# A four-layer graph attention kernel: the rows of layer 3's heads 1 to 3 from bf16 parts

## The chip, the core and the metric

The kernel runs on one core of a Trainium2 chip. The metric is the device time of one execution in microseconds (us), as the median of several runs. The core's engines are named as in the profile: PE is TensorE (matmul) and PEld its weight loads, DVE is VectorE, ACT is ScalarE, POOL is GpSimd and SP is SyncE.

## The reference

Four layers of graph attention work on 16 graphs of 1024 nodes with 256 features and an adjacency matrix. Each layer normalises x, projects it, and mixes the nodes with weights that depend on an edge's two ends. Layer 3 has four heads of 64 features:

```python
# x: (16, 1024, 256) f32; adj: (16, 1024, 1024), 0 or 1
h = jnp.maximum(_layernorm(x, axis=-1), 0.0)
# layers 0 to 2, one head each, with an activation of their own:
e = act(f1[:, :, None] + f2[:, None, :])         # f1 = Wh @ a1, f2 = Wh @ a2
attention = softmax(where(adj == 0, NEG, e))
x = x + einsum('bij,bjo->bio', attention, Wh)    # elu of it in layers 1 and 2
# layer 3, four heads (h: head, e: feature):
h = jnp.einsum('bnd,hde->bhne', x_normed, W)
weight = leaky_relu(e_src[..., :, None] + e_dst[..., None, :])
attention = softmax(where(adj == 0, NEG, weight))
out = relu(einsum('bhij,bhje->bhie', attention, h) + bias) + h
x = x + layernorm(out)                           # for each head
```

The weight of an edge (i, j) is thus a function of a number of i and a number of j. The kernel works with their exponentials, so a weight is the maximum (in one layer the minimum) of two numbers, times the mask of edges. One number runs along the partitions, the other along the free axis and has to stand on all partitions. This second one is "the row" below.

## The kernel before

The 16 graphs are called batches. Two streams run batches alternately, the even ones and the odd ones, as Python generators; a driver takes the stream that is behind by the times that the generators yield (`yield 3.6`, `yield 0.5`), and so interleaves their program order. A scheduler then orders the instructions of each engine by readiness and priority. `tc.keep_in_program_order(ins)` ties an instruction behind the one that was traced just before it on the same engine; it adds no wait on another engine. Each engine then works through its order, and waits where an input isn't there.

For every layer of a batch, and in layer 3 for every head:

- `weigh` (L306) takes the only `row` buffer in PSUM (`bufs=1`[...]), which both streams share, guarded by `row_taken`. For each of the eight blocks of 128 nodes it turns a column of 128 numbers into 128 elements of the row: one f32 transpose on PE with the column broadcast over 128 columns (L314), so that the row stands on all 128 partitions.
- It then makes eight tiles `weights` of 128x1024 on DVE (L318), each from the row, a number for each partition and a mask. The last one gives the row back.
- In layers 0 to 2, `attend` multiplies the weights with the values V (L409). `add_elu` or `finish0` evict, and `project` prepares the next layer: it centres (L274), squares on ACT (L281), transposes into a `misc` buffer in PSUM (L290), copies it to `hT` on ACT (L292), and multiplies by W (L297).

In layer 3 the columns come from `ex` (L381), which holds three groups of four heads for each block. Products go through PE in tiles of 32 columns, four side by side (L519): `add_values` for the values and `add_totals` for the sums of weights. For head 0, the values come in two blocks with `yield 3.6` behind each. Only then `weigh3(1)` begins and the row of head 1 is turned, and the totals of head 0 follow. For heads 1 to 3, the next head's row is turned before the head's own totals and values. After each head ACT copies both accumulators (L581), PE turns them back in the two `misc` buffers (L588, L596), and DVE and POOL normalise.

The lines that matter below: L88 (`ones`, used at L244 alone), L314, L318, L506 to L512 (`weigh3`), and L547 to L565, the start of the loop over heads.

Of the kernel before, what the change touches and what calls it, by code (L numbers as in the profile page):

```python
# [32 lines left out]
F32 = mybir.dt.float32  # L33
BF = mybir.dt.bfloat16
# [7 lines left out]
P = 128  # L42
# [5 lines left out]
SLOPE = 0.2  # L48
L3_SLOPE = 0.01

REACH = 75.0


# [6 lines left out]
def short_path(ctx: ExitStack, tc: tile.TileContext, ins: dict, out: bass.AP, bad: bass.AP):  # L60

    nc = tc.nc
# [22 lines left out]
    make_identity(nc, ident)  # L85
    minus_half = const.tile([P, 1], F32, name="minus_half")
    nc.vector.memset(minus_half, -0.5)
    ones = const.tile([P, P], F32, name="ones")  # L88
    nc.vector.memset(ones, 1.0)

    squares = const.tile([P, B, NI], F32, name="squares")
    inverses = const.tile([P, B, NI], F32, name="inverses")
# [69 lines left out]
    def prepare():  # L162

        forms = [
            (SLOPE, 1 - SLOPE, SLOPE - 1),
            (-SLOPE, SLOPE - 1, 1 - SLOPE),
            (0.0, 1.0, -1.0),
            (L3_SLOPE, 1 - L3_SLOPE, L3_SLOPE - 1),  # L170
        ]
        scratch = [edges.tile([P, N], F32, name="weights1") for _ in EXT]

        def extend(l: int):
            n = EXT[l] // 3
            engine = nc.vector if l == 0 else nc.gpsimd
            for c, factor in enumerate(forms[l]):
                engine.tensor_scalar_mul(
                    W[l][:, :, D + c * n : D + (c + 1) * n],
                    wa[:, :, l : l + n, 0 if c == 2 else 1],  # L180
                    factor,
                )

        def fetch(l: int):
            def begin(dst: bass.AP, src: bass.AP):
                fetched = nc.sync.dma_start(dst, src)
                if l > 0:
                    tc.keep_in_program_order(fetched)

            if l < 3:  # L190
                begin(W[l][:, :, :D], ins[f"L{l}_W"].rearrange("(k p) o -> p k o", p=P))
                begin(scratch[l][:, : 2 * D], on_all_partitions(ins[f"L{l}_a"], 2 * D))
                return
            for k in range(NK):
                begin(
                    W[3][:, k, :D].rearrange("p (h e) -> p h e", h=H),
                    ins["L3_W"][:, ts(k, P), :].rearrange("h p e -> p h e"),
                )
            for s, name in enumerate(("L3_a_src", "L3_a_dst")):
                first = ins[name]  # L200
                begin(
                    scratch[3][:, ts(s, D)].rearrange("p (h e) -> p h e", h=H),
                    bass.AP(tensor=first.tensor, offset=first.offset, ap=[[0, P], [T * E, H], [1, E]]),
                )
            for t, a in ((bias, ins["L3_bias"]), (gamma, ins["L3_gamma"]), (beta, ins["L3_beta"])):
                begin(t, on_all_partitions(a, D))

        for l in range(3):
            fetch(l)
            yield  # L210
            for k in range(NK):
                for s in range(2):
                    prod = work.tile([P, D], F32, name="above", bufs=2)
                    made = nc.vector.tensor_tensor_reduce(
                        prod, W[l][:, k, :D], scratch[l][:, ts(s, D)], op0=ALU.mult, op1=ALU.add,
                        scale=1.0, scalar=0.0, accum_out=wa[:, k, l, s : s + 1],
                    )
                    if l > 0:
                        tc.keep_in_program_order(made)
            extend(l)  # L220
            yield
        fetch(3)
        yield
        for s in range(2):
            for k in range(NK):
                prod = work.tile([P, D], F32, name="above", bufs=2)
                tc.keep_in_program_order(
                    nc.vector.tensor_mul(prod, W[3][:, k, :D], scratch[3][:, ts(s, D)])
                )
                nc.vector.tensor_reduce(  # L230
                    wa[:, k, 3:, s], prod.rearrange("p (h e) -> p h e", h=H), AX.X, ALU.add
                )
        extend(3)

        tc.keep_in_program_order(nc.vector.tensor_scalar_add(beta, beta, -2.0))
        tc.keep_in_program_order(nc.vector.tensor_scalar_mul(gamma, gamma, ROOT_E))

        groups = (3 + H) * 2
        wa2 = small.tile([P, NK, groups], F32, name="wa2", bufs=1)
        nc.vector.tensor_mul(wa2, wa.rearrange("p k g s -> p k (g s)"), wa.rearrange("p k g s -> p k (g s)"))  # L240
        norms = psum.tile([P, 3 + H, 2], F32, name="misc")
        for k in range(NK):
            nc.tensor.matmul(
                norms.rearrange("p g s -> p (g s)"), ones, wa2[:, k],  # L244
                start=(k == 0), stop=(k == NK - 1),
            )
        both = small.tile([P, 3 + H], F32, name="both", bufs=1)
        nc.vector.tensor_reduce(both, norms, AX.X, ALU.add)
        worst = small.tile([P, 1], F32, name="worst", bufs=1)
        nc.vector.tensor_reduce(worst, both, AX.X, ALU.max)  # L250
        nc.vector.tensor_scalar(bad, worst, REACH * REACH / (2.0 * D), None, op0=ALU.is_gt)
        yield
# [50 lines left out]

    row_taken = []

    def weigh(b: int, column, c, op, into: list):  # L306


        while row_taken:
            yield 0.25  # L310
        row_taken.append(b)
        r = psum.tile([P, N], F32, name="row", bufs=1)
        for i in range(NI):
            nc.tensor.transpose(r[:, ts(i, P)], column(i).to_broadcast([P, P]), ident)  # L314
        yield 0.5
        for j in range(NI):
            w = edges.tile([P, N], F32, name=f"weights{b % 2}")
            nc.vector.scalar_tensor_tensor(w, r, c(j), masks[b][:, j // 2, :, j % 2], op0=op, op1=ALU.mult)  # L318
            into.append(w)
            if j == NI - 1:  # L320
                row_taken.pop()
            yield 0.5

    def start(behind, b: int):

# [23 lines left out]
    def batch(b: int):  # L349
# [43 lines left out]
        def attend(l: int, V: bass.AP, finish, then: int):  # L393

            weights = []
            behind = weigh(
                b, lambda i: V[:, i, D + 2 : D + 3], lambda j: V[:, j, D + 1 : D + 2],
                ALU.min if l == 1 else ALU.max, weights,
            )
            yield from start(behind, b)  # L400
            following = begin(then) if then < 3 else begin3()
            steps = iter(())
            accs = {}
            sums = small.tile([P, NI], F32, name="sums_of_x")

            def product(i: int, j: int):
                if j == 0:
                    accs[i] = accumulator(b)[:, : D + 1]
                nc.tensor.matmul(  # L409
                    accs[i], weights[j][:, ts(i, P)], V[:, j, : D + 1],  # L410
                    start=(j == 0), stop=(j == NI - 1),
                )


            for j in range(NI):
                next(behind)
                product(0, j)
                product(1, j)
                if b == 0 and j == NI - 1:


                    next(preparing)
                    if l == 0:
                        next(loading[1])
                    next(preparing, None)
                yield 0.9
            for _ in behind:
                pass
            for i in range(NI):
                if i > 1:  # L430
                    for j in range(NI):
                        product(i, j)
                acc = accs.pop(i)
                finish(i, acc, sums[:, i : i + 1])
                if i != 0:
                    yield 3.6
                if i % 2 == 1:

                    yield from steps
                    steps = project(b, then, xb, sums, i // 2, following[1])  # L440
                yield from islice(steps, 1)
            yield 1.0
            yield from steps
            return following[0]
# [61 lines left out]
        def weigh3(h: int):  # L506
            if h == H:
                return iter(())
            return weigh(
                b, lambda i: ex[:, i, 2 * H + h : 2 * H + h + 1],  # L510
                lambda j: ex[:, j, H + h : H + h + 1], ALU.max, weights,
            )  # L512

# [32 lines left out]

        behind = weigh3(0)  # L547
        yield from start(behind, b)
        for h in range(H):


# [2 lines left out]
            if h == 0:  # L554
# [6 lines left out]
                    yield 3.6  # L561
                for _ in behind:
                    pass
            behind = weigh3(h + 1)
            yield from start(behind, b)  # L565

# [447 lines left out]
```

## Time and profile before

| | before |
|---|---|
| time, median of 3 runs | 2988.73 us (2987.17 to 2989.75) |
| f32 turns for rows, layers 0 to 2 | 384, 273 ns median in the records |
| f32 turns for rows, layer 3 | 512, 273 ns median |
| weight loads of these turns | 137 ns median |
| one tile of weights on DVE | 1275 ns median |
| TensorE clock granted | 0.99 of full speed |

The records of matmuls overlap[...]. How long PE is taken up is read from the distance of two starts instead. For the f32 turns in one row this distance is 109 ns, less than half of the 273 ns in the record. The first one of a group has to wait for its own weight load.

The timeline, the windows and the chain of waits give the rest: the first shows when each row is made and what follows it, the second which engine is full in a stretch, and the third what the end depends on.

### The profile page before, as it was taken

How to read it: one execution, taken by the hardware profiler on the slowest of the kernel's cores; microseconds unless marked ns; L12 is line 12 of the kernel's file. 1: busy time of each engine (PE TensorE's matmuls, PEld its weight loads, DVE VectorE, ACT ScalarE, POOL GpSimd, SP SyncE). 2: the span in 40 equal slices, each digit the busy share in tenths (PEclk: the TensorE clock that was granted, in tenths of full speed). 3: DMA queues.
4: the chain of work that ended last, by engine and by line, in shares of the span. 5: the costliest groups of instructions: out<-in, count | busy, mean ns of one | idle time of the engine just before them, and what ended most of it. 6: DMA issues, size and time to landing. Idle time of an engine off the chain costs nothing.

```text
span 2988.9 us, 44636 instructions
## 1 busy us (share of the span) xinstructions
PE 2839.7 (95%) x16774; PEld 1986.1 (66%) x16774; DVE 2148.9 (72%) x4467; ACT 1090.0 (36%) x3009; POOL 956.7 (32%) x1455
## 2 busy tenths in 40 slices
PE   7999999999999999999999999999999999999985
PEld 5775856768576685766758566685766857667552
DVE  5658688585976859678586885859768586785855
ACT  2333434343343433424334243433434334343331
POOL 2123324243242423424233242432424233242333
PEclk9999999999999999999999999999999999999987
DMA  7204122040221303122041220302213031110101
GB/s 122 39 8 60 33 29 57 8 50 29 30 56 17 55 16 50 36 29 57 5 51 32 29 57 8 50 29 32 55 17 59 11 50 36 15 29 6 25 18 26
DMA packets 120495, 106.11 MB, mean 36 GB/s; under 512 B 73680, under 2 KB 91216, under 8 KB 120272
## 3 DMA queue, kind: packets, MB, share of 16 engines
q0 software_dynamic: 40448, 67.12, 15.4%
q1 hardware_dynamic: 79824, 36.05, 5.8%
q8 instruction: 135, 2.21, 0.3%
q14 instruction: 88, 0.72, 0.1%
HBM read 153.49 MB, written 33.55 MB: 63 GB/s over the span
## 4 chain that ended last, share of the span: by engine, by line
PE 55%; DVE 28%; issue 8%; POOL 5%; ACT 3%; DMA 1%; POOLq 0%; SPq 0%; ACTq 0%; DVEq 0%
PE acc L409 33%; DVE weights L318 19%; PE acc L297 9%; PE acc L519 9%; PE misc L290 2%; POOL rstd L261 2%; POOL y L487 1%; ACT square L281 1%; DVE x_b L345 1%; DVE V L365 1%; PE row L314 1%; DVE x_b L344 1%; ACT below L341 1%; DVE y L488 1%; DVE var L496 1%
## 5 line engine op out<-in xcount | busy, mean ns | idle before, releaser
L409 PE MATMUL acc<-V,weights 128*128 128x257 f32 x6144 | 1436.6, 385 | 26.2 <-DVE weights L318 15.7
L409 PEld LDWEIGHTS acc<-V,weights 128*128 128x128 f32 x6144 | 1143.3, 191 | 262.0 <-DVE weights L318 68.5
L318 DVE SCALAR_TENSOR_TENSOR weights<-row,ex,mask 128x1024 f32<-128x1024 f32 x512 | 630.3, 1273 | 102.5 <-PE row L314 95.7
L519 PE MATMUL acc<-weights,V 128*32 128x512 f32 x6144 | 692.1, 597 | 11.4 <-DVE weights L318 7.5
L297 PE MATMUL acc<-W,hT 128*128 128x259 f32 (+1 forms) x2048 | 521.6, 391 | 40.4 <-ACT hT L292 28.9
L297 PEld LDWEIGHTS acc<-W,hT 128*128 128x128 f32 x2048 | 379.0, 191 | 148.3 <-ACT hT L292 35.1
L318 DVE SCALAR_TENSOR_TENSOR weights<-row,V,mask 128x1024 f32<-128x1024 f32 x384 | 473.9, 1275 | 0.7 <-PE row L314 0.7
L519 PEld LDWEIGHTS acc<-weights,V 128*32 128x32 f32 x6144 | 189.4, 110 | 422.9 <-issue 415.3
L341 ACT ACTIVATE below<-acc,inv 128x256 f32<-128x256 f32 x256 | 120.8, 472 | 798.9 <-DVE inv L334 559.5
L281 ACT ACTIVATE square<-x_b,minus_mean 128x256 bf16<-128x256 f32 x512 | 259.7, 507 | 230.8 <-DVE minus_mean L271 155.0
L261 POOL TENSOR_TENSOR rstd<-rstd,minus_half 128x2 f32<-128x2 f32 (+1 forms) x320 | 302.0, 944 | 20.3
L389 POOL TENSOR_TENSOR x_b<-x_b,beta 128x256 f32<-128x256 f32 x128 | 93.4, 730 | 490.9 <-ACT square L281 490.9
L260 POOL TENSOR_SCALAR rstd<-squared 128x2 f32<-128x2 f32 x256 | 57.7, 225 | 573.2 <-ACT square L281 572.3
L333 DVE TENSOR_SCALAR inv<-acc 128x1 f32<-128x1 f32 x256 | 39.3, 154 | 277.6 <-PE acc L409 276.4
L344 DVE SCALAR_TENSOR_TENSOR x_b<-below,x_b 128x256 f32<-128x256 f32 x256 | 136.8, 534 | 82.7 <-ACT below L341 82.5
L292 ACT ACTIVATE hT<-misc 128x512 f32<-128x512 f32 x256 | 150.0, 592 | 119.9 <-PE misc L290 119.5
L361 ACT ACTIVATE V<-acc,rstd 128x3 f32<-128x3 f32 x384 | 98.5, 262 | 251.7 <-PE acc L297 250.8
L581 ACT COPY sums<-acc 128x512 f32<-128x512 f32 x128 | 74.8, 585 | 278.6 <-PE acc L519 278.6
L365 DVE TENSOR_SCALAR V<-acc,rstd,V 128x256 f32<-128x256 f32 x256 | 131.7, 538 | 62.2 <-ACT V L361 61.3
L290 PE MATMUL misc<-ident,centered 128*128 128x128 f32 x1024 | 158.7, 277 | 15.7 <-DVE centered L274 13.9
L274 DVE TENSOR_SCALAR centered<-x_b,minus_mean 128x256 f32<-128x256 f32 x512 | 168.5, 357 | 5.2
L290 PEld LDWEIGHTS misc<-ident,centered 128*128 128x128 f32 x1024 | 121.3, 141 | 60.1 <-issue 26.9
(76 smaller groups left out, 2218.1 us busy)
## 6 DMA issues: line engine op xcount, KB each, us to landing
adj_i<-in_adj_dram POOLq DMA_DIRECT2D x128, 256.0 KB, 3.9
x_b<-in_x_dram SPq DMA_DIRECT2D x16, 1024.0 KB, 6.4
narrow<-in_adj_dram POOLq DMA_DIRECT2D x64, 256.0 KB, 9.3
out_dram<-y POOLq DMA_DIRECT2D x32, 512.0 KB, 7.4
mask<-narrow SPq DMA_TRANSPOSE x64, 4.4
W<-in_L_gnn_W_dram SPq DMA_DIRECT2D x3, 256.0 KB, 7.2
weights<-in_L_gnn_a_dram SPq DMA_DIRECT2D x3, 256.0 KB, 8.5
W<-in_L_gnn_W_dram SPq DMA_DIRECT2D x2, 128.0 KB, 8.2
```

The costliest lines, as they stand in the source:

```text
L261: nc.gpsimd.tensor_tensor(r, r, minus_half.to_broadcast([P, n]), op=ALU.pow)
L274: nc.vector.tensor_scalar(centered[:, n, :], xb[:, 2 * pair + n, :], minus_mean[:, n : n + 1], 0.0, op0=ALU.add, op1=ALU.max,)
L281: nc.scalar.activation(square, xb[:, 2 * pair + n, :], AF.Square, bias=minus_mean[:, n : n + 1], accum_out=squared[:, n : n + 1],)
L290: nc.tensor.transpose(turned[:, k, ts(n, P)], centered[:, n, ts(k, P)], ident)
L292: nc.scalar.mul(hT, turned, ROOT_D)
L297: nc.tensor.matmul(projected, hT[:, k, ts(n, P)], W[l][:, k, :], start=(k == 0), stop=(k == NK - 1),)
L318: nc.vector.scalar_tensor_tensor(w, r, c(j), masks[b][:, j // 2, :, j % 2], op0=op, op1=ALU.mult)
L341: nc.scalar.activation(below, acc[:, :D], AF.Exp, scale=inv)
L344: nc.vector.scalar_tensor_tensor(xi, below, 1.0, xi, op0=ALU.min, op1=ALU.add)
L365: nc.vector.tensor_scalar(V[:, i, :D], projected[:, :D], rstd, V[:, i, D : D + 1], op0=ALU.mult, op1=ALU.mult,)
L409: nc.tensor.matmul(accs[i], weights[j][:, ts(i, P)], V[:, j, : D + 1], start=(j == 0), stop=(j == NI - 1),)
L519: made = nc.tensor.matmul(accT[ts(n, QUAD), :], values, moving, start=first, stop=last)
```

## The change

The rows of heads 1, 2 and 3 of layer 3 are no longer turned from f32 columns one block at a time. Once a batch, right after head 0's row, POOL multiplies the four heads' columns by 65536 and splits them into three bf16 parts whose sum is the f32 number again: the rounded number, the rounded rest, and the rest of that. They stand in a tile of 128 x 96: 3 parts x 8 blocks x 4 heads. One bf16 transpose on PE turns the 96 columns into 96 rows of 128 elements, held in order behind head 0's values, and ACT copies the result to SBUF.

A block of a head's row is then one bf16 matmul. Its weights are a column of the constant `rows_of` that is broadcast over 128 columns; it has 1/65536 at the three partitions that belong to this head and block, so the matmul adds the three parts up in f32 and puts the sum on all partitions. The aim is that PE works on bf16 instead of f32 for these rows. Head 0's row and those of layers 0 to 2 stay as they are. The constant `ones` shrinks to one column that is broadcast where it is used.

```diff
+THIRDS = 65536.0
...
-    ones = const.tile([P, P], F32, name="ones")
+    ones = const.tile([P, 1], F32, name="ones")
     nc.vector.memset(ones, 1.0)
+    rows_of = const.tile([3 * QUAD, QUAD], BF, name="rows_of")
+    for t in range(3):
+        nc.vector.tensor_scalar_mul(
+            rows_of[ts(t, QUAD), :], ident[ts(t, QUAD), ts(t, QUAD)], 1.0 / THIRDS
+        )
+    ident_bf = const.tile([P, P], BF, name="ident_bf")
+    nc.vector.tensor_copy(ident_bf, ident)
...
-                norms.rearrange("p g s -> p (g s)"), ones, wa2[:, k],
+                norms.rearrange("p g s -> p (g s)"), ones.to_broadcast([P, P]), wa2[:, k],
...
-    def weigh(b: int, column, c, op, into: list):
+    def weigh(b: int, turn, c, op, into: list):
...
-            nc.tensor.transpose(r[:, ts(i, P)], column(i).to_broadcast([P, P]), ident)
+            turn(r[:, ts(i, P)], i)
...
+    def along_row(column):
+        return lambda r, i: nc.tensor.transpose(r, column(i).to_broadcast([P, P]), ident)
...
+            def from_thirds(r: bass.AP, i: int):
+                m = i * H + h
+                row = rows_of[:, m : m + 1].to_broadcast([3 * QUAD, P])
+                nc.tensor.matmul(r, row, thirds_T, start=True, stop=True)
             return weigh(
-                b, lambda i: ex[:, i, 2 * H + h : 2 * H + h + 1],
+                b, from_thirds if h > 0 else along_row(lambda i: ex[:, i, 2 * H : 2 * H + 1]),
                 lambda j: ex[:, j, H + h : H + h + 1], ALU.max, weights,
             )
...
         behind = weigh3(0)
         yield from start(behind, b)
+        rest = small.tile([P, NI, H], F32, name="rest", bufs=1)
+        nc.gpsimd.tensor_scalar_mul(rest, ex[:, :, 2 * H :], THIRDS)
+        thirds = small.tile([P, 3, NI, H], BF, name="thirds", bufs=1)
+        nc.gpsimd.tensor_copy(thirds[:, 0], rest)
+        nc.gpsimd.tensor_sub(rest, rest, thirds[:, 0])
+        nc.gpsimd.tensor_copy(thirds[:, 1], rest)
+        nc.gpsimd.tensor_sub(thirds[:, 2], rest, thirds[:, 1])
         for h in range(H):
...
                 for _ in behind:
                     pass
+                turned_thirds = psum.tile([3 * QUAD, P], BF, name="misc")
+                made = nc.tensor.transpose(
+                    turned_thirds, thirds.rearrange("p t i h -> p (t i h)"), ident_bf
+                )
+                tc.keep_in_program_order(made)
+                thirds_T = small.tile([3 * QUAD, P], BF, name="thirds_T", bufs=1)
+                nc.scalar.copy(thirds_T, turned_thirds)
             behind = weigh3(h + 1)
             yield from start(behind, b)
```

More of the change, by code (lines that the diff above doesn't have):

```diff
@@ L396, in attend @@
             behind = weigh(
-                b, lambda i: V[:, i, D + 2 : D + 3], lambda j: V[:, j, D + 1 : D + 2],
+                b, along_row(lambda i: V[:, i, D + 2 : D + 3]), lambda j: V[:, j, D + 1 : D + 2],
                 ALU.min if l == 1 else ALU.max, weights,
```

## Prediction

> **What bounds the kernel now.** I read the page first, for the shares of the engines and the chain of the work that ended last.
>
> ```profile
> PE 2839.7 (95%) x16774; PEld 1986.1 (66%) x16774; DVE 2148.9 (72%) x4467; ACT 1090.0 (36%) x3009; POOL 956.7 (32%) x1455
> PE 55%; DVE 28%; issue 8%; POOL 5%; ACT 3%; DMA 1%; POOLq 0%; SPq 0%; ACTq 0%; DVEq 0%
> ```
>
> TensorE is busy for 95%, yet 28% of the chain is VectorE. So the bound changes by stage. The starts of head 0's row (L314 on `ex`) show the rhythm: 1291.2, 1472.5, 1653.9 us and so on, one batch every 181.3 us, with the two streams taking turns. I cut one period into three windows, at the first DVE instruction that uses head 1's row (1489.6) and at the PE restart behind head 3's row (1531.5).
>
> ```profile
> 1454.20:1489.60 35.40, 35.14 (x216) 24.98 (x215) 18.04 (x42) 10.79 (x32) 7.31 (x16) 1.00 0.00 0
> 1489.60:1531.50 41.90, 39.78 (x274) 22.25 (x272) 40.83 (x61) 12.05 (x28) 11.78 (x15) 1.00 0.46 51
> 1531.50:1635.50 104.00, 101.21 (x562) 76.20 (x563) 74.93 (x175) 45.13 (x130) 40.98 (x59) 1.00 0.22 41
> ```
>
> The columns are the length, then busy PE, PEld, DVE, ACT and POOL. The first and third windows belong to PE (35.14 of 35.40, 101.21 of 104.00). The middle one belongs to DVE, 40.83 of 41.90. Heads 1, 2 and 3 make their rows at the start, inside and at the end of that middle window, so each row has to be judged where it stands.
>
> Head 1, from the timeline:
>
> ```profile
> 1482.18 1.15 PE L297 MATMUL acc<-W,hT 128*128 128x259 f32 x4
> 1483.26 5.36 PE L519 MATMUL acc<-weights,V 128*32 128x512 f32 x48
> 1483.36 0.26 ACT L361 ACTIVATE V<-acc,rstd 128x3 f32<-128x3 f32 x1 [4.66 <-PE acc L297]
> 1484.83 0.51 ACT L281 ACTIVATE square<-x_b,minus_mean 128x256 bf16<-128x256 f32 x1 [1.21 <-DVE minus_mean L271]
> 1488.54 1.09 PE L314 MATMUL row<-ident,ex 128*128 128x128 f32 x8
> 1489.67 1.28 DVE L318 SCALAR_TENSOR_TENSOR weights<-row,ex,mask 128x1024 f32<-128x1024 f32 x1 [4.28 <-PE row L314]
> ```
>
> PE streams without a hole, DVE stands idle for 4.28 us until the row is there, and then hardly pauses for 41.9 us. Head 1's row is on the path in full.
>
> Head 2:
>
> ```profile
> 1514.82 1.04 PE L314 MATMUL row<-ident,ex 128*128 128x128 f32 x8
> 1515.93 2.25 PEld L409 LDWEIGHTS acc<-V,weights 128*128 128x128 f32 x11 [0.31 <-ACT above L343]
> 1517.99 1.27 DVE L318 SCALAR_TENSOR_TENSOR weights<-row,ex,mask 128x1024 f32<-128x1024 f32 x1
> ```
>
> The row is finished 2.1 us before DVE gets to it, and the next PE work waits for an ACT eviction anyway. Head 2's row fills a hole.
>
> Head 3:
>
> ```profile
> 1529.84 0.73 PE L314 MATMUL row<-ident,ex 128*128 128x128 f32 x5 [0.40 <-DVE inv L333]
> 1530.88 0.59 ACT L292 ACTIVATE hT<-misc 128x512 f32<-128x512 f32 x1
> 1531.53 0.66 PE L596 MATMUL misc<-ident,sums 128*128 128x128 f32 x4 [0.96 <-ACT hT L292]
> 1532.02 0.49 PE L314 MATMUL row<-ident,ex 128*128 128x128 f32 x3
> 1533.16 1.23 DVE L318 SCALAR_TENSOR_TENSOR weights<-row,ex,mask 128x1024 f32<-128x1024 f32 x1
> ```
>
> Five of the eight turns stand ahead of a wait for ACT's `hT`, and only the last three delay PE behind it.
>
> **What the Trainium skill says.** (1) "TensorE: Matmul & The Clock Gate", section "Wait — 56ns, not 53.3ns?": a warm bf16 matmul starts N/2.4 + 2.5 ns after the one before, 55.6 ns for N = 128. The trace agrees with its form: f32 transposes start 109 ns apart, twice 53.3 ns plus 2.3; no bf16 matmul is in this trace. (2) The same page, "Back-to-back issue gap": in a stream of weight loads and matmuls, N = 128 holds about 81 ns each. Nothing here shows it. (3) The same page, "Weight-path perf modes — Fast Weight Load (FWL) and DoubleRow": loads of 128 columns that aren't f32 can be faster. That would help, but I don't count on it.
>
> **The change part by part.**
>
> *A row (48 of them, heads 1 to 3 of 16 batches).* It takes away eight f32 transposes and puts eight bf16 matmuls of the same 128 columns there. The first f32 turn of a group takes 160 ns to the next start, with its weight load in front, and the others 109 ns: 160 + 7 x 109 = 923 ns. The load takes 137 ns in the records against 191 ns for an f32 matmul's and 110 ns for 32 columns at L519. These three fit 84 ns of latency plus columns x passes / 2.4 (one pass for the turn, two for the f32 matmuls), so a load of 128 columns occupies its path for about 53 ns and starts 2 ns after the matmul before it. A bf16 matmul would then be spaced at 53 + 5 = 58 ns; the bounds are 56 and 81 ns by the skill, and 109 ns if nothing is gained. I take 58, because it follows from this trace's loads: 109 + 7 x 58 = 515 ns, so 0.41 us less for a row (0.22 at 81 ns).
>
> *Where this counts.* Head 1: all of it, 0.41. Head 2: nothing, since the wait for `above` grows by what the row loses. Head 3: three turns of 51 ns, 0.15. The last batch runs alone and its heads 2 and 3 count more; I add 0.8 us once.
>
> *The turn of the parts (16).* One bf16 transpose a batch. No row of before shows it; between 0.06 us (its stream alone) and 0.3 us (if it parts a run of L519, whose change to other work and back costs 0.13 + 0.09 in the timeline). `keep_in_program_order` ties it to the PE instruction traced just before it. This isn't a matmul of the values: at the yield behind the second half of the values the other stream traces its projection, the L297 that runs at 1482.18. So the turn can go between it and the L519 at 1483.26, where the change of shape is paid anyway. I take 0.10.
>
> *The wait that it brings.* Head 1's row now waits for turn, ACT copy, PE. The copy has 128 elements: between L361 (3 elements, 262 ns) and L341 (256, 472 ns), some 0.37 us. In ACT's queue are V at 1483.36 and the squares, which end at 1486.07; behind either one the copy is done by 1486.5, and the row is issued at 1488.54. Some 2 us of slack, so nothing. What would queue behind a late row are the other stream's four turns at 1489.47 and the rest of the totals; DVE waits for the row itself.
>
> *POOL, five operations of 128x32 a batch.* Between 205 ns (128x4 copy, L388) and 614 ns (128x256, L384), so 1.0 to 3.1 us. POOL is free from 1474.06 until 1486.15. Nothing. The `misc` buffer that the turn takes is back after its copy, before the next transposes at 1489.47. The constants are five short DVE instructions in place of one larger `memset`, at the start, under the first loads. `ones` as a broadcast column feeds the same four matmuls. Nothing for either.
>
> *The sum.* 15 periods x (0.41 - 0.10 + 0.15) + 0.8 = 7.7 us: 2988.7 - 7.7 = 2981.0.
>
> **The rivals.**
>
> A, *the full saving*: the new order of work moves rows 2 and 3 out of the holes, or fills these. 48 x 0.41 - 16 x 0.1 = 18 us, 2971. For it: PE is at 95%. Against it: the two holes stand in all periods alike, and DVE is 97% busy between them.
>
> B, *the weight load binds*: 81 ns. 15 x (0.22 - 0.10 + 0.08) + 0.4 = 3.4 us, 2985.3; at 109 ns it ends at about 2990. For it: the figure in the skill for pairs. Against it: no load here is longer than its matmul's stream.
>
> C, *a new wait ahead of head 1's row*: slower. If the copy stands in ACT's queue behind the copy of the sums (L581, released at 1488.68, 0.58 us), it ends at about 1489.7 with its handovers, so the row comes 1.2 us later, and DVE, which has waited for it 4.28 us, waits on. 16 x (1.2 + 0.1 - 0.41 - 0.15) = 11.8 us: 3000.5. With a test square of 1.15 us in front as well, 3019. For it: ACT works strictly through a queue shared by two streams, and this row opens the stretch that DVE bounds. Against it: the squares' end at 1486.07 leaves over 2 us of an empty ACT.
>
> **How the numbers follow.** The forecast 0.42, A 0.16, B 0.21, C 0.21. Only the faster cases reach below 2982.7, 0.2% under before: most of the forecast (0.38) and A, so 0.54 faster. Same: B and the rest of the forecast, 0.25. Slower: C, 0.21. The range goes from a little beyond A (2968) to the near part of C (2997); what is left out is the far part of C and a reordering that helps more than A.
>
> **What would show it.** Starts of the bf16 matmuls 56 to 60 ns apart; head 1's first weights about 0.3 us nearer to the start of the L519 run; a period of about 180.8 us; the wait behind head 2's row grown to 0.6 us; no idle PE ahead of head 1's row. Wrong if the bf16 spacing is 80 ns or more, if head 1's row waits for the ACT copy, or if PE's order around the three rows isn't that of before.

## The result, and the profile after

The changed kernel takes 2950.12 us (2949.25 to 2950.81) against 2988.61 us: a ratio of 0.9873 with a 95% interval of 0.9858 to 0.9887, so 38.5 us less. The forecast was 7.7 us less and its range ended at 2968. The rivals of the prediction didn't reach so far either: the one with the full saving on PE gave 18 us.

The page of the changed kernel, its engines and the chain of waits:

```profile
PE 2810.6 (95%) x16790; PEld 1969.3 (67%) x16790; DVE 2124.8 (72%) x4471; ACT 1092.1 (37%) x3025; POOL 980.7 (33%) x1535
PE 60%; DVE 23%; issue 8%; POOL 5%; ACT 3%; DMA 1%; POOLq 0%; SPq 0%; ACTq 0%; DVEq 0%
```

PE's busy time falls by 29 us, but DVE's falls by 24.1 us too, and the change takes no work from DVE. Its share of the chain goes from 28 to 23%. That is the first sign that something other than the rows has changed. Next, the groups of the new instructions (name, number, duration min/median/max in ns, first and last start):

```profile
L529 PEld LDWEIGHTS <-rows_of x384: 94/98/101, 213.2 to 2895.1; 96*128 96x128 bf16 x192
L529 PE MATMUL row<-thirds_T,rows_of x384: 216/219/231, 213.2 to 2895.1; 96*128 96x128 bf16 x192
L600 ACT COPY thirds_T<-misc x16: 248/250/264, 208.1 to 2867.9; 96x128 bf16<-96x128 bf16 x16
L595 PEld LDWEIGHTS <-thirds x16: 120/122/123, 207.5 to 2867.3; 128*96 128x96 bf16 x16
```

The starts of two of these matmuls in a row lie 56 ns apart (median), in place of 109. The period, by the starts of head 0's row, is 178.88 us instead of 181.34: 2.46 us less, and 15 periods of that are 36.9 us. The following windows cut a period at DVE's first use of head 1's row and at the start of head 3's row (columns as in the prediction). First the kernel before, from head 1 on, then the changed kernel with the window ahead of head 1's row as well:

```profile
1489.60:1529.80 40.20, 39.05 (x269) 21.73 (x267) 39.15 (x56) 11.06 (x25) 11.78 (x15) 1.00 0.48 53
1529.80:1635.50 105.70, 101.94 (x567) 76.71 (x568) 76.61 (x179) 46.12 (x132) 40.98 (x59) 1.00 0.22 41
```

```profile
1253.00:1288.40 35.40, 35.14 (x219) 25.06 (x218) 18.07 (x45) 10.56 (x33) 8.42 (x21) 1.00 0.00 1
1288.40:1328.00 39.60, 38.40 (x269) 21.36 (x268) 38.72 (x57) 11.43 (x26) 11.80 (x15) 1.00 0.49 54
1328.00:1431.90 103.90, 101.13 (x569) 76.40 (x567) 75.43 (x179) 46.17 (x132) 41.37 (x59) 1.00 0.19 41
```

The stretch behind head 3's row has lost 1.8 us, more than the others, although only its first half microsecond is the row. Now the three rows in turn, from the timeline of the changed kernel. Head 1:

```profile
1282.29 0.22 PE L595 MATMUL misc<-ident_bf,thirds 128*96 128x128 bf16 x1
1282.65 0.25 ACT L600 COPY thirds_T<-misc 96x128 bf16<-96x128 bf16 x1
1287.73 0.62 PE L529 MATMUL row<-thirds_T,rows_of 96*128 96x128 bf16 x8
1288.18 0.61 PE L301 MATMUL misc<-ident,centered 128*128 128x128 f32 x4
1288.39 1.28 DVE L330 SCALAR_TENSOR_TENSOR weights<-row,ex,mask 128x1024 f32<-128x1024 f32 x1 [3.87 <-PE row L529]
```

This is what was forecast. The turn of the parts sits between the L308 and the L541, its copy ends at 1282.90, almost 5 us before the row wants it, and the row takes PE for 0.45 us (1287.73 to 1288.18) instead of 0.93. Head 2:

```profile
1313.54 0.61 PE L529 MATMUL row<-thirds_T,rows_of 96*128 96x128 bf16 x8
1314.27 1.12 DVE L359 SCALAR_TENSOR_TENSOR x_b<-below,x_b 128x256 f32<-128x256 f32 x1 [0.17 <-ACT below L356]
1314.65 3.33 PEld L424 LDWEIGHTS acc<-V,weights 128*128 128x128 f32 x16 [0.67 <-ACT above L358]
1315.18 1.34 POOL L517 TENSOR_TENSOR y<-y,x_b 128x512 f32<-128x512 f32 x1
1315.32 3.65 DVE L330 SCALAR_TENSOR_TENSOR weights<-row,ex,mask 128x1024 f32<-128x1024 f32 x3
1320.08 0.41 DVE L360 SCALAR_TENSOR_TENSOR x_b<-above,x_b 128x256 f32<-128x256 f32 x1
```

The wait of PE's weight loads behind the row has grown from 0.31 to 0.67 us, much as forecast. But DVE's order is another one. Before, the eviction `x_b<-above` of the other stream stood ahead of head 2's weights, beside a POOL operation:

```profile
1516.44 1.34 POOL L502 TENSOR_TENSOR y<-y,x_b 128x512 f32<-128x512 f32 x1
1516.76 1.30 DVE L345 SCALAR_TENSOR_TENSOR x_b<-above,x_b 128x256 f32<-128x256 f32 x1
```

It took 1.30 us there. Now four tiles of weights go first, and the same eviction takes 0.41 us. The weights don't get longer beside POOL. In the whole trace of before, all 31 of these evictions that take over 0.8 us run beside POOL's `y<-y,x_b`, and the 192 that run beside no POOL work stay under 0.45 us. From the start of `x_b<-below` to the first weights, 2.44 us have become 1.05. The Trainium skill ("GPSIMD Engine Reference", section "1. Specifications") says that POOL's way to SBUF is shared with VectorE and that instructions with two SBUF inputs contend: `above` and `x_b` are two, while the weights read their row from PSUM. The trace agrees with both sides of that. Head 3:

```profile
1328.00 0.61 PE L529 MATMUL row<-thirds_T,rows_of 96*128 96x128 bf16 x8
1328.54 5.36 PE L541 MATMUL acc<-weights,V 128*32 128x512 f32 x48
1333.83 0.44 PE L633 MATMUL misc<-ident,sums 128*128 128x128 f32 x2
```

Before, five turns of the row were followed by the turn of the sums, which waited 1.12 us for `hT` (with 0.11 us counted for each turn; the profile's records of matmuls run on longer, so it gives 0.96). Now the row is in one piece, and a block of 48 passes of head 2's totals and values stands in front of the sums, whose buffer is long free by 1333.83. The wait is gone, and so is the one ahead of the row, 0.56 us by the same count (0.40 in the profile).

So there are two theories. **O**: the gain is mainly another order of work on the engines; with the bf16 rows the scheduler made other choices, and the kernel's time follows these. **P**: the gain is the shorter rows, with PE as the bound.

### The profile page after: what moved, and what is told of

Read it like the earlier page. It is cut to its first block, busy times and chain, and to the rows that moved or that the text cites. A ratio compares the mean times of both kernels' runs of the same rounds, so it can differ in the third digit from the quotient of the medians.

```text
span 2948.4 us, 44754 instructions
## 1 busy us (share of the span) xinstructions
PE 2810.6 (95%) x16790; PEld 1969.3 (67%) x16790; DVE 2124.8 (72%) x4471; ACT 1092.1 (37%) x3025; POOL 980.7 (33%) x1535
## 4 chain that ended last, share of the span: by engine, by line
PE 60%; DVE 23%; issue 8%; POOL 5%; ACT 3%; DMA 1%; POOLq 0%; SPq 0%; ACTq 0%; DVEq 0%
PE acc L424 36%; DVE weights L330 16%; PE acc L541 11%; PE acc L308 9%; PE misc L301 2%; POOL rstd L272 2%; POOL y L502 2%; ACT square L292 1%; DVE V L380 1%; PE row L337 1%; DVE y L503 1%; DVE var L511 1%; DVE y L507 1%; DVE mean L505 1%; ACT below L356 1%
## 5 line engine op out<-in xcount | busy, mean ns | idle before, releaser
L541 PE MATMUL acc<-weights,V 128*32 128x512 f32 x6144 | 692.0, 597 | 12.1 <-DVE weights L330 8.1
L308 PE MATMUL acc<-W,hT 128*128 128x259 f32 (+1 forms) x2048 | 516.5, 389 | 41.7 <-ACT hT L303 29.2
L308 PEld LDWEIGHTS acc<-W,hT 128*128 128x128 f32 x2048 | 379.6, 191 | 138.0 <-ACT hT L303 47.1
L541 PEld LDWEIGHTS acc<-weights,V 128*32 128x32 f32 x6144 | 189.6, 110 | 417.6 <-issue 410.7
L271 POOL TENSOR_SCALAR rstd<-squared 128x2 f32<-128x2 f32 x256 | 64.6, 253 | 462.8 <-ACT square L292 461.9
L285 DVE TENSOR_SCALAR centered<-x_b,minus_mean 128x256 f32<-128x256 f32 x512 | 182.6, 385 | 5.3
L149 POOL DMA_DIRECT2D adj_i<-in_adj_dram x128 | 74.7, 584 | 286.4 <-ACT adj_i L154 254.9
```

The lines of the kernel that those rows point to most:

```text
L285: nc.vector.tensor_scalar(centered[:, n, :], xb[:, 2 * pair + n, :], minus_mean[:, n : n + 1], 0.0, op0=ALU.add, op1=ALU.max,)
L308: nc.tensor.matmul(projected, hT[:, k, ts(n, P)], W[l][:, k, :], start=(k == 0), stop=(k == NK - 1),)
L541: made = nc.tensor.matmul(accT[ts(n, QUAD), :], values, moving, start=first, stop=last)
```

## The experiments

The table has the median time of each run, and from its trace the mean distance between the starts of the rows of heads 0 to 3 and of the next batch's head 0 (seven batches) and the period (eight), all in us. "Before" was 2988.4 to 2989.7 us beside these runs. The means also hold batches in which the granted clock fell to half for 3.4 us: one each in the traces of e4 and e10, and most of e15's. Where that matters, the text gives a usual batch instead.

| kernel | time | 0 to 1 | 1 to 2 | 2 to 3 | 3 to next 0 | period |
|---|---|---|---|---|---|---|
| before | 2988.6 | 16.02 | 26.28 | 15.03 | 124.02 | 181.34 |
| changed | 2950.1 | 16.07 | 25.85 | 14.46 | 122.52 | 178.88 |
| e1 parts unread | 2989.8 | 16.07 | 26.28 | 15.04 | 124.12 | 181.50 |
| e2 head 1 alone | 2986.3 | 16.07 | 25.81 | 15.04 | 124.13 | 181.05 |
| e3 head 2 alone | 2977.0 | 16.07 | 26.28 | 14.50 | 123.51 | 180.35 |
| e4 head 3 alone | 2985.1 | 16.07 | 26.31 | 14.95 | 124.00 | 181.29 |
| e5 heads 2 and 3 | 2954.7 | 16.07 | 26.31 | 14.46 | 122.53 | 179.35 |
| e6 f32, eviction tied | 2971.5 | 16.01 | 26.28 | 14.46 | 123.39 | 180.14 |
| e7 f32, PE tied by hand | 3003.6 | 16.01 | 26.28 | 15.02 | 125.13 | 182.44 |
| e8 f32, both by hand | 2986.1 | 16.01 | 26.28 | 14.46 | 124.42 | 181.19 |
| e9 f32, order of changed | 2964.3 | 16.07 | 26.31 | 14.46 | 122.95 | 179.78 |
| e10 bf16, order of before | 2984.2 | 16.07 | 25.82 | 14.95 | 124.32 | 181.12 |
| e11 turn not held | 2948.0 | 16.02 | 25.85 | 14.46 | 122.53 | 178.84 |
| e12 row 1 earlier | 2968.9 | 12.62 | 30.18 | 14.46 | 122.54 | 179.79 |
| e13 row 1 earlier, whole | 2927.1 | 12.58 | 28.01 | 14.46 | 122.53 | 177.57 |
| e14 f32, PE's order of changed | 3006.5 | 16.07 | 26.32 | 15.04 | 125.24 | 182.65 |
| e15 f32, DVE's order of changed | 3008.8 | 16.07 | 26.28 | 14.46 | 126.24 | 183.16 |

### One head at a time (e1 to e5)

The condition in `weigh3` chooses which heads read the parts; e1 has the empty set, e2, e3 and e4 one head each, e5 two:

```diff
-                b, from_thirds if h > 0 else along_row(lambda i: ex[:, i, 2 * H : 2 * H + 1]),
+                b, from_thirds if h in (1,) else along_row(lambda i: ex[:, i, 2 * H + h : 2 * H + h + 1]),
```

> The split on POOL, its turn and the ACT copy stay, but all rows are made from f32 columns as before, so nothing reads the parts. Theory O (the gain comes from two places where the scheduler chose another order) and theory P (the gain is PE time spared by the bf16 rows) both expect the added path to be hidden but for about 0.06 us of PE a batch: 2989.6 us. If the gain lay in the added work or the constants, this would be near 2950.

Measured: 2989.78 us, ratio 1.0004 (0.9996 to 1.0013). The added path is hidden.

> Only head 1's row from the parts. O: both orders are those of before, so just 0.41 us of the row less 0.06 of the turn for each of 16 batches: 2983 us, a period of 180.9 us. P: a third of the gain: 2976 us.

Measured: 2986.31 us, ratio 0.9993 (0.9984 to 1.0002). From head 1 to head 2 the row's 0.47 us are seen in full, and the period is 0.45 us below e1. The time is nearer to before than either theory said, but its interval reaches to no difference, so the interval of the rows is the better witness. P's third of the gain isn't there.

> Only head 2's row from the parts. O: the weights of head 2 now go ahead of the other stream's eviction in DVE's order, as in the changed kernel; that takes some 1 us off the stretch that DVE bounds: 2973 us, and the eviction (x_b<-above) that took 1.30 us takes 0.42 us. P: a third of the gain, 2976 us, by PE; my sum on record expected nothing of this head, 2989.6 us.

Measured: 2977.04 us, ratio 0.9960 (0.9946 to 0.9974). It brings the most of the three heads, though its row filled a hole. The program has the weights ahead of the eviction; the long evictions (over 0.8 us) fall from 31 to 16 of 256, as they do in the changed kernel (15). The period is 1.15 us below e1: 0.54 from head 2 to head 3, and 0.61 behind head 3.

> Only head 3's row from the parts. O: the row is in one piece, but the turn of the sums behind it still waits for hT, since the tiles of the totals do not go in front of it: three turns of 0.11 us leave the path, 2984 us. P: a third of the gain, 2976 us.

Measured: 2985.13 us, ratio 0.9989 (0.9982 to 0.9996). The usual period is 181.08 us against e1's 181.42, so three turns of 0.11 us, as O had it; the mean in the table holds one batch of 182.58 us, whose clock fell. The wait for `hT` is still there.

> Rows of heads 2 and 3 from the parts, head 1's from f32. Heads alone gave 2977.0 (head 2) and 2985.1 (head 3) against 2988.4. If their gains add (P), 2973.8 us. O: with both, the second block of head 2's totals and values goes in front of the turn of the sums, which fills the wait for hT (0.56 + 1.12 us a period): 2953 us, a period of about 179.0 us.

Measured: 2954.69 us, ratio 0.9889 (0.9873 to 0.9906). Heads 2 and 3 alone save 11.4 and 3.3 us, together 33.7. Savings of PE time would add up. Only with both heads does the block of totals and values come ahead of the turn of the sums, and only then do the last 1.0 us behind head 3 go (123.51 to 122.53). Head 3's shorter row is part of that step; e9 below parts the two.

### f32 rows in another order (e6 to e8)

No bf16 and no parts: the kernel before, with some instructions tied to others by edges that set the order of issue alone.

```diff
+            if h == 2 and j == 3:  # weights of head 2
+                hold["weights"] = made
...
-        nc.vector.scalar_tensor_tensor(
+        last = nc.vector.scalar_tensor_tensor(
             xi, above, 0.0, xi, op0=ALU.add, op1=ALU.add, accum_out=total
         )
+        if "weights" in hold:
+            behind_of(last, hold.pop("weights"))
```

> All rows from f32 as before; one thing is changed: the eviction x_b<-above of the other stream is tied behind the fourth tile of head 2's weights in DVE's order. O: the gain of head 2 alone without any bf16: 2977 us. P: 2988.4 us.

Measured: 2971.51 us, ratio 0.9944 (0.9927 to 0.9961). One edge for each batch gives 17 us with every row as it was, and the intervals from head 2 on shrink as in e3. The edge is all that was written; the scheduler answered it with some other moves on PE, DVE and ACT, so the 17 us are the edge's with what followed from it. That is more than twice the gain that the prediction gave to the whole change.

```diff
+                if h == 2 and first == 4:
+                    for back in turns:             # turns of head 1's sums
+                        behind_of(back, pinned[-1])
...
+                if urgent:                         # first of head 2's second block
+                    behind_of(made, urgent.pop())  # behind head 3's row, at high priority
```

> All rows from f32 as before; one thing is changed: head 3's row stays in one piece, the second block of head 2's totals and values goes right behind it, and the turn of head 1's sums goes behind that. O: the waits of 1.12 us behind five turns of the row are filled, 16 x 1.1 us: 2971 us. P: 2988.4 us.

Measured: 3003.62 us, ratio 1.0051 (1.0034 to 1.0068), slower than before, and against both theories. The table has the loss behind head 3: 125.13 us against 124.02.

> All rows from f32 as before, with the two orders of the runs before in one kernel, so that PE's and DVE's order are nearly those of the changed kernel without its bf16 matmuls. O: all but what the shorter rows themselves give, which is 0.41 us at head 1 and some 0.4 at head 3, less 0.06: 2950.1 + 16 x 0.75 = 2962 us. P: 2988.4 us.

Measured: 2986.14 us, ratio 0.9992 (0.9986 to 0.9999): 24 us above what O asked for. PE's order was nearly that of the changed kernel (198 of its 16774 places differ), but the scheduler had ordered DVE, ACT and POOL in its own way around it (363 of DVE's 4467 places differ; between before and the changed kernel it is 535). So O could only be tested with the order of all engines.

### The whole order against the rows (e9, e10)

Both programs trace the same instructions in number and order, so that an order can be carried over by name. Each engine's instructions are tied one behind the other:

```diff
+def pin(tc):
+    named = {i.name: i for i in tc.nc.cur_bb.bb.instructions}
...
+    for order in orders:  # for each engine, the names in the other program's order
+        for early, late in zip(order, order[1:]):
+            tc.add_manual_dep(named[late], early, info, reason="order")
```

> All rows from f32 columns (the split, its turn and the copy stay, unread), but every engine's instructions are tied into the exact order that they have in the changed kernel. Two hand-made orders before this one failed to bring the gain, and their traces show that DVE, ACT and POOL had taken other orders behind them. Theory O (the gain is the order of all engines): the period of the changed kernel, 178.88 us, plus 0.46 us for head 1's row and about 0.4 for head 3's: 2964 us. Theory P (bf16 time on PE, the order is worth little): 2985 us or more.

Measured: 2964.32 us, ratio 0.9917 (0.9901 to 0.9934).

> The changed kernel's instructions, all tied into the exact order that they have with f32 rows (that of the kernel with the parts unread, whose period is that of before). O: my sum on record, which kept the order: 0.41 us at head 1, nothing at head 2, 0.15 us at head 3, less the turn: 2981 us, a period of 180.8 us. P: close to the changed kernel, 2950 to 2960 us.

Measured: 2984.21 us, ratio 0.9985 (0.9978 to 0.9992).

Together with e1 and the changed kernel this is a square:

| | order of f32 rows | order of the changed kernel |
|---|---|---|
| f32 rows | 2989.8 (e1) | 2964.3 (e9) |
| bf16 rows | 2984.2 (e10) | 2950.1 (changed) |

The order gives 25.5 us with f32 rows and 34.1 us with bf16 rows. The rows give 5.6 us in the old order and 14.2 us in the new one. So O is shown for the larger part of the gain, and P holds for the smaller. The traces have the orders as intended: e9's engines work in the changed kernel's order and e10's in that of e1, which is that of before with the parts added. The changed kernel tied to its own order was not run, so what the edges themselves cost is not measured; but e9 differs from the changed kernel's intervals only by the rows of head 1 (0.46 us) and head 3 (0.43 us).

By intervals, the 2.62 us a period from e1 to the changed kernel fall, but for 0.02, into four parts: 1.15 us with the weights of head 2 ahead of the eviction (e3 against e1), 0.56 us with the block in front of the sums (behind head 3, e3's 123.51 us against e9's 122.95), and the two rows, 0.46 and 0.43. The square shows the order as a whole. That these two places carry it is read from the intervals and the timelines; e6 shows the first of them by itself, and for the second no edge written by hand brought the gain.

The timeline of e10 has the old picture at heads 2 and 3, with the bf16 rows in it:

```profile
1513.44 1.29 DVE L410 SCALAR_TENSOR_TENSOR x_b<-above,x_b 128x256 f32<-128x256 f32 x1
1514.66 2.47 DVE L380 SCALAR_TENSOR_TENSOR weights<-row,ex,mask 128x1024 f32<-128x1024 f32 x2
```

```profile
1526.42 0.45 PE L579 MATMUL row<-thirds_T,rows_of 96*128 96x128 bf16 x5 [0.32 <-DVE inv L398]
1528.20 0.66 PE L683 MATMUL misc<-ident,sums 128*128 128x128 f32 x4 [1.32 <-ACT hT L353]
1528.69 0.33 PE L579 MATMUL row<-thirds_T,rows_of 96*128 96x128 bf16 x3
```

The eviction is long again, and the wait for `hT` has grown from 0.96 us to 1.32: it takes up what the five shorter turns ahead of it gave. Behind this wait, in one batch of e10's trace, the granted clock was half for 3.4 us, and that batch took 182.63 us. The usual period is 180.85 us, which is what O asked for (180.8).

### One engine's order (e14, e15)

As e9, with the list of PE alone or of DVE alone.

> All rows from f32 columns, PE's instructions tied into the exact order of the changed kernel; the scheduler orders the other engines, and puts DVE's eviction x_b<-above ahead of head 2's weights as before. If PE's order carries the gain: 2966 to 2970 us. If the order of DVE does, and PE's adds only on top of it: 2980 to 2990 us.

Measured: 3006.54 us, ratio 1.0060 (1.0043 to 1.0076), above both ranges.

> All rows from f32 columns, DVE's instructions tied into the exact order of the changed kernel; PE keeps two turns of head 3's row ahead of the sums and six behind them. If DVE's order carries the gain: 2972 us, as when the one eviction was tied by hand (2971.5), plus 1 us for the turn. If PE's order is needed: over 2980 us.

Measured: 3008.78 us, ratio 1.0067 (1.0050 to 1.0084).

Neither engine's order carries the gain alone; with the others ordered by the scheduler, the kernel is 17 and 19 us slower than e1. The timeline of e14, some 20 us behind head 3's row:

```profile
1555.99 0.69 DVE L546 TENSOR_TENSOR y<-y,rstd 128x512 f32<-128x512 f32 x1 [2.13 <-POOL rstd L303]
1558.42 0.66 PE L664 MATMUL misc<-ident,sums 128*128 128x128 f32 x4 [0.96 <-ACT hT L334]
1560.98 1.14 PE L339 MATMUL acc<-W,hT 128*128 128x259 f32 x4 [1.03 <-ACT above L389]
```

Head 1's normalisation has come late; DVE waits for POOL's `rstd` with the other stream's eviction queued behind it, ACT waits for that eviction's number, and PE for ACT. In the changed kernel this chain runs earlier and PE hardly waits there: over eight batches PE waits 9.9 us for `above` ahead of L339's matmuls in e14, and 1.7 us ahead of the same matmuls in the changed kernel. With 9.6 us, e7 and e8 have this wait too.

e15 loses its time otherwise. In thirteen batches PE waits 1.9 us for ACT's V, some 25 us behind head 3's row, a wait that neither e1 nor the changed kernel has there. In nine of the thirteen the granted clock is then half for 3.4 us (0.51 from 1195.3 to 1198.7 us, right behind such a wait that ended at 1194.62), and these nine take 183.7 to 183.9 us; the others take 182.1. So some 1.7 us of such a batch is the clock. Why it falls behind the wait in some batches and not in others isn't shown.

### The held turn, and head 1's row (e11 to e13)

```diff
-                tc.keep_in_program_order(made)
```

> The changed kernel without the line that ties the turn of the parts behind the instruction before it; the turn then goes into the run of head 0's values, ahead of their second block. If the tie matters for waits (POOL's split not done, ACT's copy in the way), slower by 1 us a period, 2966 us. My reading of the trace: POOL has ended its split 3 us before, so only the change of shape inside the run, 0.2 us a period, is paid: 2953 us.

Measured: 2948.02 us, ratio 0.9860 (0.9843 to 0.9876), an interval that overlaps with the changed kernel's. The period is 0.04 us shorter, so the tie is worth next to nothing. The turn doesn't go where it was expected: in the trace it stands ahead of the first block of head 0's values, behind L308, and so parts no run.

In e12 the row matmuls of head 1 have high priority:

```diff
-                nc.tensor.matmul(r, row, thirds_T, start=True, stop=True)
+                with tc.high_priority() if h == 1 else nullcontext():
+                    nc.tensor.matmul(r, row, thirds_T, start=True, stop=True)
```

> The changed kernel with head 1's eight row matmuls at high priority, so that they go ahead of the second half of head 0's second block of values. In the changed kernel DVE idles for 3.87 us ahead of this row and then works almost without a break for 40 us. If that idle time is on the path, the period falls by 1.5 to 2.5 us, as far as PE's own work allows: 2910 to 2926 us. If PE is the only bound there, only the two extra changes of shape are seen, 2957 us.

Measured: 2968.93 us, ratio 0.9932 (0.9915 to 0.9948), 19 us slower than the changed kernel and outside both expectations. The row is 3.4 us earlier, but the way from head 1 to head 2 is 4.3 us longer. PE's timeline shows why:

```profile
1469.12 1.04 PE L542 MATMUL acc<-weights,V 128*32 128x512 f32 x2
1470.10 0.23 PE L530 MATMUL row<-thirds_T,rows_of 96*128 96x128 bf16 x1
1470.26 1.04 PE L542 MATMUL acc<-weights,V 128*32 128x512 f32 x2
```

Two passes of one column tile, cut off from the other three, hold PE from 1469.12 to 1470.10, 0.98 us; in an uncut run eight passes of four tiles take 0.86. So e13 moves the row as a whole between two blocks, on top of e11:

```diff
+            if h == 0:  # the second block of values behind the last matmul of row 1
+                behind_of(second[0], row1[-1])
```

> The changed kernel with head 1's eight row matmuls in one piece ahead of head 0's second block of values (that block is tied behind them; the turn of the parts isn't tied). In the run before, the row stood inside the block, and twice a pair of PE passes ran alone where four column tiles run side by side, about 0.95 us each. If DVE's idle time ahead of the row is on the path and only those cuts hid it: a period of 177 to 178 us, 2920 to 2935 us. If PE bounds this stretch once the row is early, and the idle time is just slack: 2948 to 2952 us.

Measured: 2927.13 us, ratio 0.9793 (0.9776 to 0.9809). It is the fastest kernel of the study, 61 us below before, 23 us below the changed kernel, and 21 us below e11, from which its source differs by the place of the row alone. DVE's idle time ahead of head 1's row falls to 0.38 us, and the other stream's matmuls, which waited 0.60 us for DVE's weights in the kernels before and after (at 1511.47 and 1310.19), run through:

```profile
1454.55 1.28 DVE L330 SCALAR_TENSOR_TENSOR weights<-row,ex,mask 128x1024 f32<-128x1024 f32 x1 [0.38 <-PE row L536]
1474.87 7.21 PE L424 MATMUL acc<-V,weights 128*128 128x257 f32 x32
```

Of the 3.5 us by which the row is earlier, 1.3 us reach the period. From there to head 3's row PE is busy for 41.60 of 42.10 us and DVE for 39.33, so PE is now the bound of this stretch too.

## Why the prediction was wrong

**Which engine bounds which stretch: right.** Head 1's row was on the path in full (e2: 0.47 us from head 1 to head 2), and e13 shows that DVE's idle time ahead of it was worth something.

**The spacing of the bf16 matmuls: right in size.** 56 ns, where 58 was taken; rival B with its 81 ns is out. (B's 0.22 us counts 137 ns for the first matmul of a row, the forecast's 0.41 counts 109; with 109 in both, B would have 0.25.) The first of head 1's row takes 66 ns to the next start, not 109, so this row gives 0.47 us and not 0.41. Only head 1's f32 row began with 160 ns; for heads 0 and 2 the first turn took 109 ns like the others, so there the first one had no wait for its load, and head 3's row gives 0.43 us where it counts in full.

The loads take 98 ns, against 137 for the f32 turns. The section "Weight-path perf modes — Fast Weight Load (FWL) and DoubleRow" of "TensorE: Matmul & The Clock Gate" in the Trainium skill, which the prediction cited but didn't count on, agrees: 128 bf16 columns load faster (98 ns) than the 96 of the parts' turn (122 ns). By the form of the prediction's sum 84 + 96/2.4 = 124 ns fits the latter at normal speed, and 98 leaves about 14 ns for 128 columns. The two loads differ in more than their columns, though (one is a broadcast column of 96 partitions), and no run parts these.

**The turn, the copy, POOL: right.** e1 is 1.4 us above before with an interval that includes no change; its usual period is 181.42 us against 181.33 before, where 0.10 us was taken for the turn. Rival C fell: almost 5 us lie between the copy and its use.

**"Where this counts": the step that failed.** It put the new durations into the old order: head 1 0.41 us, head 2 nothing, head 3 three turns, 7.7 us in all, and had no term for a change of order. In the old order the sum is right: e10's usual period is 180.85 us, and the sum's was 180.8. The time of e10, 2984.2 us, is 3 us above the 2981.0 on record; a batch with a fallen clock made 1.8 us of that in the trace, and the rest is not settled.

But the order isn't part of the source: the scheduler chooses it when the program is built. With head 2's row from the parts its weights passed an eviction (1.15 us a period), and with head 3's row from the parts as well, a block of PE work passed a turn that waits (0.56 us), which also let head 3's row count in full (0.43 us). By times, the order makes 25.5 us with f32 rows and 34.1 us with bf16 rows. That the new rows are what changed the scheduler's choices follows from e1 to e5, where the choices change with the heads. What in them did it, the shorter matmuls or their other inputs, and by how little the choice was tipped, hasn't been tried.

**Rival A: right in kind, wrong in its limit.** It named a new order that moves rows or fills holes, but held the gain to the PE time that the rows free, 18 us. The rows do give 14.2 us in the new order. But that order also removed waits (0.56 and 1.12 us a period) and made a DVE operation shorter (1.30 to 0.41 us), and neither is PE time of a row. The prediction named a changed order of PE as a thing that would make it wrong, and left out of its range a reordering that helps more than A. PE's order did change; DVE's, which it didn't name, gave more of the gain.

## What to carry to other kernels

Where a scheduler fixes the order, the price of a change is the price of its instructions plus that of a new order, and here the second was the larger one: compare the order of the two programs before explaining a difference by durations. A square of two orders and two sets of instructions separates them, while tying one engine's order alone misled here, since the others fell out of step. Look at the holes of the profile for what an edge in the order could do by itself: one tied eviction gave 17 us, and one row moved ahead of a block 21 us. A mean over batches can hide a clock that falls in some of them, so look at the batches one by one.

## What the hardware showed beyond this

An eviction on DVE with two SBUF inputs took 1.30 us beside a POOL operation of 1.34 us, and 0.41 us away from it; beside POOL's small `rstd` operations it also stayed at 0.42 us. DVE instructions with the row in PSUM as an input stayed at 1.27 us in both places. A column tile's two passes cut out of a run of four tiles cost 0.98 us, more than all eight passes of four tiles side by side (0.86). In e15 a wait of PE of 1.9 us was followed in nine batches of thirteen by 3.4 us at half the granted clock, at a price of some 1.7 us each.
